# Cross-attention with 20 heads: the score tile from one product of 308 columns and two of 154, with a new order of steps in the slot

## The chip, the core and the metric

The kernel runs on one core of a Trainium2 chip. The metric is the device time of one execution, in microseconds (us). In what follows PE is TensorE, DVE is VectorE, ACT is ScalarE, POOL is GpSimd and SP is SyncE, whose queue issues the kernel's DMAs. PEld are the weight loads of TensorE.

## The reference

There are 32 batch elements, each with 512 query rows of 640 channels (`x`) and 77 context rows of 1024 channels. 20 heads have 32 channels each. Only the text part of the context has keys (77 of them), so the other three attentions of the full reference have no columns and add nothing.

```
q = heads(x @ to_q_w);  k = heads(ctx @ to_k_w);  v = heads(ctx @ to_v_w)
p = softmax(q @ k^T / sqrt(32))            # 512 x 77 for each head
out = merge(p @ v) @ to_out_w + to_out_b + x
```

All arrays are fp32.

## The kernel before

**Numbers in two parts.** TensorE multiplies in a shortened fp32 format (`fp32r`). To keep the accuracy, each operand is held as a high part and a low part: `split` (L100) copies the value into the shortened format on ACT (L101) and subtracts that copy from the value on DVE (L102). A product is then three TensorE products, high by high, high by low and low by high (`PAIRS`, L120), added up in PSUM.

**Stages.** A prologue computes keys and values for all 2464 context rows in five groups of up to 512 rows (`context`, `keys`, `context_values`, L133 to L208), and stores them with both parts in DRAM (`k_dram`, `v_dram`). The instructions of this prologue are ordered by a scheduler. The main part is written in a fixed order (`manual_schedule`, L657): what stands first in the program stands first on its engine's queue, and each engine works its queue in order.

**Slots.** The main part goes through 160 slots. Slot `n` belongs to batch element `b` and block `j` of four heads (five blocks in a batch element, `b, j = divmod(n, 5)`). `slot` (L523) mixes the work of several blocks so that TensorE always has something to do. For a block `n` these steps exist:

- `queries` (L316): 15 products of 512 columns give the transposed queries of the block, in one PSUM bank `pq`. `split_q` (L330) makes the high and low part `qt` of them: one ACT copy, one DVE subtraction. Both are done one slot ahead.
- `scores` (L334): for each of the four tiles of 128 query rows, three products of 308 columns (four heads of 77 keys). The moving operand `kb` holds the keys of each head in that head's 32 rows and zeros elsewhere, for both parts. After them DVE takes the maximum of each head (L348). There are three PSUM buffers for these tiles.
- `exps` (L353): four exponentials a tile on ACT (L358), with their sums.
- One slot later, `sums` (L366, a reciprocal on DVE), `normalize` (L371, a multiplication on POOL), and `transpose_p` (L377): a DVE transpose in 32 x 32 blocks into `z`, and four DMAs that write `z` to a DRAM tile `pd`.
- `load_p` (L393) reads `pd` back in the transposed layout as `raw`; three slots after the scores, `cast_p` (L400, ACT) and `rest_p` (L407: an ACT copy, a DVE subtraction at L411 with both operands in SBUF, a POOL subtraction at L414) make its two parts `pp`.
- `values` (L422): 8 products of 512 columns into `pa`, then `split_a` (L436).
- `piece` (L472) does 12 products of 320 columns of the output projection of the batch element before, twice a slot; `finish` (L480) adds residual and bias on DVE (L486) and stores the rows. `add_bias` (L450) adds the bias to the loaded residual on POOL.
- For the next batch element, `load_x` (L256) loads the rows, `transpose_x` (L264) transposes a quarter of them on DVE, and `split_x` (L268) makes the two parts of one of five blocks of channels: an ACT copy (L273) and a POOL subtraction (L274). Tables say in which slot of the five and at which of three places this is done: `TRANSPOSE_X` (L504) and `SPLIT_X` (L505).
- `refill` (L512) loads the keys and values of a batch element, in two groups of blocks (`load_keys` L295, `load_values` L304).

The order of the slot's steps by engine, before the change: DVE does the reciprocal, the first maximum, the subtraction of `rest_p`, the second maximum, output additions if there are any, the third maximum, the subtraction of `split_q`, the transpose of `p`, output additions, the fourth maximum and the subtraction of `split_a`. POOL does the subtraction of `rest_p`, `normalize`, the bias and the splits of `x`. From slot 4 on `values` are done, from slot 5 on the output projection. `end` (L594) finishes the last blocks.

Of the kernel before, what the change touches and what calls it, by code (L numbers as in the profile page):

```python
# [23 lines left out]
P = 128  # L24
# [26 lines left out]
def kernel(  # L51
# [22 lines left out]


    nc = tc.nc
    B, S, C = x.shape
# [83 lines left out]
    def keys(g0, gn, j, k):  # L161
        if k == 0:
            pks[j] = psk.tile([P, G], F32, tag="ps", name="pk")
        for n, (a, c) in enumerate(PAIRS):
            nc.tensor.matmul(  # L165
                pks[j][:, :gn],
                wk_s[:, k, a, j * P : (j + 1) * P],
                cts[k][:, c, :gn],
                start=(k == 0 and n == 0),
                stop=(k == NK - 1 and n == 2),  # L170
            )
        if k == NK - 1:
            pk = pks.pop(j)
            ks = kvt.tile([P, 2, G], FPR, tag="ks", name="ks")
            split(ks[:, 0, :gn], ks[:, 1, :gn], pk[:, :gn])
            nc.sync.dma_start(
                k_dram[:, j, :, g0 : g0 + gn].bitcast(F32), ks[:, :, :gn].bitcast(F32)
            )

# [88 lines left out]
    def split_x(b, c, engine=nc.gpsimd):  # L268

        xt = main.tile([P, 2, S], FPR, tag="xt", name="xt", bufs=8)  # L270
        src = xss[b].rearrange("p (a t) u -> p t a u", t=NQ)[:, :, :, c * Q : (c + 1) * Q]
        parts = [xt[:, i, :].rearrange("p (t a j) -> p t a j", t=NQ, j=Q) for i in range(2)]
        nc.scalar.copy(parts[0], src)  # L273
        engine.tensor_tensor(parts[1], src, parts[0].bitcast(F32), ALU.subtract)  # L274
        xts[b, c] = xt
# [4 lines left out]
    for g, (j0, nj) in enumerate(GROUPS):  # L280
        kb = main.tile([P, nj, 2, KCOLS], FPR, name=f"kb{g}")
        nc.gpsimd.memset(kb.bitcast(F32), 0.0)
        kbs.append(kb)
# [4 lines left out]
    qts = [main.tile([P, 2, S], FPR, name=f"qt{n}") for n in range(2)]  # L288
    z = main.tile([P, NBLK, NQ, Q], F32, name="z")
# [5 lines left out]
    def load_keys(b, g):  # L295
        j0, nj = GROUPS[g]
        for i in range(HPC):
            r = slice(i * HD, (i + 1) * HD)
            nc.sync.dma_start(
                kbs[g][r, :, :, i * NKEY : (i + 1) * NKEY].bitcast(F32),  # L300
                k_dram[r, j0 : j0 + nj, :, b * NKEY : (b + 1) * NKEY].bitcast(F32),
            )

    def load_values(b, g):  # L304
# [25 lines left out]
    def split_q(n):  # L330
        qt = qts[n % 2]
        split(qt[:, 0, :], qt[:, 1, :], pqs.pop(n))

    def scores(n, t):  # L334
        b, j = divmod(n, NC_)
        g = GROUP_OF[j]
        qt, kb = qts[n % 2], kbs[g][:, j - GROUPS[g][0]]
        sc = ps.tile([P, S], F32, tag="sc", name="sc", bufs=3)
        for m, (a, c) in enumerate(PAIRS):
            nc.tensor.matmul(  # L340
                sc[:, :KCOLS],
                qt[:, a, t * P : (t + 1) * P],
                kb[:, c, :],
                start=(m == 0),
                stop=(m == 2),
            )
# [89 lines left out]
    def split_a(n):  # L436
        if n >= N - NC_ + 1:
            at = main.tile([P, 2, S], FPR, tag="xt", name="at", bufs=8)
# [64 lines left out]
    BIAS = {2: (1, 0), 3: (1, 1), 4: (1, 2), 0: (2, 3)}  # L503
    TRANSPOSE_X = {0: ((), (0,), (1,)), 1: ((2,), (3,), ())}  # L504
    SPLIT_X = {1: ((), (0,)), 2: ((1,), (2,)), 3: ((3,), (4,))}  # L505
    wos = []
# [5 lines left out]
    def refill(b, j):  # L512

        if j == 0 and b >= 1:
            load_keys(b, 1)
        elif j == 1 and b >= 1:
            load_values(b, 0)
        elif j == 2 and b + 1 < B:
            load_keys(b + 1, 0)
        elif j == 3 and b >= 1:  # L520
            load_values(b, 1)

    def slot(n, beside=None):  # L523
# [133 lines left out]
    with tc.manual_schedule(engines=ENGINES):  # L657
        g0, gn = GROUPS_KV[-1]
        load_x(0)
        load_keys(0, 0)  # L660
        load_keys(0, 1)
        for g in range(2):
            load_values(0, g)
        for h in range(2):
# [69 lines left out]
```

## Time and profile before

| what | value |
|---|---|
| median of 3 runs | 2028.63 us (2027.86 to 2028.84) |
| the profiled execution's own time | 2028.15 us |
| its span, first to last instruction | 2026.0 us |
| mean granted TensorE clock | 0.991 of full speed |
| score products (L340) | 1920 of 308 columns, 377.8 us busy |
| projection products (L458) | 3840 of 320 columns, 615.9 us busy |
| query products (L322) | 2400 of 512 columns, 610.9 us busy |
| normalize (L373, POOL) | 160, mean 2276 ns |
| subtraction of rest_p (L411, DVE / L414, POOL) | 160 each, mean 1226 / 1770 ns |
| transpose of p (L380, DVE) | 160, mean 1511 ns |
| subtraction of split_q (L102, DVE) | 160, mean 684 ns |
| DMA over the span | 417.14 MB, mean 206 GB/s |

The page gives one execution. A busy time is the sum of an engine's instruction durations without overlaps, a mean is the duration of one instruction. The durations of matmuls overlap, since TensorE takes up the next before the last has drained, so their means are not their pace. In the timeline a line has the start, the duration, the engine, the line of the code, the operation with the tile it writes and the tiles it reads, the shapes, the count, and in brackets the engine's idle time just before, with what ended it.

### The profile page before, as it was taken

The numbers are of one execution on the slowest core, as the hardware profiler recorded it, in microseconds if no ns is written. First come the engines' busy times: TensorE is split into PE (matmuls) and PEld (weight loads), VectorE is DVE, ScalarE is ACT, GpSimd is POOL, SyncE is SP. The second block draws the span as 40 slices with busy tenths as digits, with TensorE's granted clock in tenths as the row PEclk, the third lists the DMA queues.
The fourth block names the chain that finished last, engine by engine and source line by source line (L and its number), as shares of the span: only waits on it lengthen the run. The fifth ranks groups of instructions, "written<-read, shape, count | busy, mean of one in ns | idle before, by whom it ended". The sixth has DMA issues, their size and how long they took to land.

```text
span 2026.0 us, 37077 instructions
## 1 busy us (share of the span) xinstructions
PE 1990.2 (98%) x11012; PEld 1802.7 (89%) x11012; DVE 1253.3 (62%) x1999; ACT 1397.0 (69%) x6057; POOL 1051.7 (52%) x615
## 2 busy tenths in 40 slices
PE   8899997999999999999999999999999999999998
PEld 7799986899999999999999999999999999999997
DVE  5443235566666666666666666666666666666663
ACT  3322127777778777777777777777778777787772
POOL 0000024666666666666656566666666666666654
PEclk9999998999999999999999999999999999999999
DMA  7963267988888888888888888888888887888865
GB/s 188 250 217 99 103 151 167 230 211 218 219 219 218 211 220 217 214 215 221 218 216 219 210 223 207 216 216 222 218 215 211 214 216 214 220 215 216 221 187 157
DMA packets 530212, 417.14 MB, mean 206 GB/s; under 512 B 144415, under 2 KB 433725, under 8 KB 530013
## 3 DMA queue, kind: packets, MB, share of 16 engines
q1 hardware_dynamic: 530013, 414.77, 78.7%
q8 instruction: 90, 1.47, 0.3%
q14 instruction: 109, 0.89, 0.1%
HBM read 239.30 MB, written 175.32 MB: 205 GB/s over the span
## 4 chain that ended last, share of the span: by engine, by line
PE 92%; DMA 3%; SPq 1%; ACT 1%; DVE 1%; issue 0%; POOL 0%; DVEq 0%; ACTq 0%; POOLq 0%
PE po L458 28%; PE pq L322 27%; PE pa L428 15%; PE sc L340 13%; PE pk L165 5%; PE pv L191 5%; DMA cs<-in_ctx_dram 1%; ACT pn L358 1%; DMA raw<-pd 0%; SPq L149 0%; SPq L111 0%; DVE z L380 0%; DMA xs<-in_x_dram 0%; DMA wraw<-in_L_xattn_to_out_w_dram 0%; SPq L387 0%
## 5 line engine op out<-in xcount | busy, mean ns | idle before, releaser
L358 ACT ACTIVATE pn<-sc,nm 128x77 f32<-128x77 f32 x2560 | 799.4, 329 | 105.1 <-DVE nm L348 101.4
L458 PE MATMUL po<-wo_s,at 128*128 128x320 f32 x3840 | 615.9, 310 | 5.2 <-DVE xr L486 5.2
L322 PE MATMUL pq<-xt,wq_s 128*128 128x512 f32 x2400 | 610.9, 395 | 0.0
L458 PEld LDWEIGHTS po<-wo_s,at 128*128 128x128 f32 x3840 | 576.5, 188 | 5.8 <-DVE xr L486 5.5
L414 POOL TENSOR_TENSOR pp<-raw,pp 64x512 fp32r<-64x512 f32 x160 | 283.2, 1770 | 512.5 <-ACT pp L410 510.0
L358 ACT ACTIVATION_READ_ACCUMULATOR pn<-sc,nm 128x1 f32 x2560 | 530.3, 207 | 0.0
L322 PEld LDWEIGHTS pq<-xt,wq_s 128*128 128x128 f32 x2400 | 437.3, 188 | 79.8
L348 DVE TENSOR_REDUCE nm<-sc 128x4 f32<-128x308 f32 x640 | 299.7, 469 | 297.0 <-PE sc L340 294.9
L373 POOL TENSOR_TENSOR pn<-pn,rs 128x1232 f32<-128x1232 f32 x160 | 364.1, 2276 | 33.1 <-DVE rs L368 20.9
L340 PE MATMUL sc<-kb,qt 128*128 128x308 f32 x1920 | 377.8, 306 | 2.4 <-ACT qt L101 1.7
L340 PEld LDWEIGHTS sc<-kb,qt 128*128 128x128 f32 x1920 | 325.4, 188 | 45.2 <-ACT qt L101 2.4
L428 PE MATMUL pa<-pp,vb 128*128 128x512 f32 x1280 | 331.5, 401 | 10.7 <-ACT pp L404 9.5
L380 DVE STREAM_TRANSPOSE z<-pn 128x1280 f32<-128x1280 f32 x160 | 241.8, 1511 | 78.8 <-POOL pn L373 29.4
L428 PEld LDWEIGHTS pa<-pp,vb 128*128 128x128 f32 x1280 | 246.0, 198 | 49.9 <-ACT pp L404 10.0
L274 POOL TENSOR_TENSOR xt<-xs,xt 128x512 fp32r<-128x512 f32 x157 | 202.6, 1294 | 149.0 <-ACT xt L273 145.6
L101 ACT CAST at<-pa 128x512 fp32r<-128x512 f32 x160 | 94.0, 588 | 256.8 <-PE pa L428 256.6
L411 DVE TENSOR_TENSOR pp<-raw,pp 128x1024 fp32r<-128x1024 f32 x160 | 196.1, 1226 | 50.6 <-ACT pp L404 50.3
L451 POOL TENSOR_TENSOR xr<-xr,bias 128x640 f32<-128x640 f32 x128 | 201.4, 1574 | 1.8 <-DMA xr<-in_x_dram 1.7
L404 ACT CAST pp<-raw 128x1024 fp32r<-128x1024 f32 x160 | 169.4, 1059 | 5.3 <-DMA raw<-pd 4.9
L165 PE MATMUL pk<-ct,wk_s 128*128 128x512 f32 (+1 forms) x600 | 137.8, 391 | 9.8 <-ACT ct L101 9.8
L191 PE MATMUL pv<-wv_s,ct 128*128 128x320 f32 (+1 forms) x960 | 143.6, 311 | 1.8 <-DVE vs L102 1.8
L191 PEld LDWEIGHTS pv<-wv_s,ct 128*128 128x128 f32 (+1 forms) x960 | 140.9, 186 | 4.0 <-DVE vs L102 2.1
(37 smaller groups left out, 1099.1 us busy)
## 6 DMA issues: line engine op xcount, KB each, us to landing
pd<-z SPq DMA_DIRECT2D x640, 160.0 KB, 3.8
raw<-pd SPq DMA_DIRECT2D x160, 512.0 KB, 4.2
xs<-in_x_dram SPq DMA_DIRECT2D x128, 320.0 KB, 7.5
xr<-in_x_dram SPq DMA_DIRECT2D x128, 320.0 KB, 4.7
out_dram<-xr SPq DMA_DIRECT2D x128, 320.0 KB, 3.5
raw<-pd SPq DMA_DIRECT2D x160, 128.0 KB, 4.4
v_dram<-vs SPq DMA_DIRECT2D x19, 640.0 KB, 3.7
k_dram<-ks SPq DMA_DIRECT2D x20, 512.0 KB, 3.3
```

The lines of the kernel that those rows point to most:

```text
L165: nc.tensor.matmul(pks[j][:, :gn], wk_s[:, k, a, j * P : (j + 1) * P], cts[k][:, c, :gn], start=(k == 0 and n == 0), stop=(k == NK - 1 and ...
L191: nc.tensor.matmul(pv[:tn, :HALF], cts[k][:, a, t0 : t0 + tn], wv_s[:, k, c, h * HALF : (h + 1) * HALF], start=(k == 0 and n == 0), stop=( ...
L274: engine.tensor_tensor(parts[1], src, parts[0].bitcast(F32), ALU.subtract)
L322: nc.tensor.matmul(pqs[n], wq_s[:, k, a, j * P : (j + 1) * P], xts[b, k][:, c, :], start=(k == 0 and m == 0), stop=(k == NC_ - 1 and m == 2),)
L340: nc.tensor.matmul(sc[:, :KCOLS], qt[:, a, t * P : (t + 1) * P], kb[:, c, :], start=(m == 0), stop=(m == 2),)
L348: nc.vector.tensor_reduce(nm, sc[:, :KCOLS].rearrange("p (h k) -> p h k", k=NKEY), AX.X, ALU.max, negate=True)
L358: nc.scalar.activation(pnb[n % 2][:, at, :NKEY], sc[:, i * NKEY : (i + 1) * NKEY], AF.Exp, bias=nm[:, i : i + 1], accum_out=sms[n][:, at : ...
L373: nc.gpsimd.tensor_tensor(pf, pf, rs.unsqueeze(2).to_broadcast([P, NQ * HPC, NKEY]), ALU.mult)
L380: nc.vector.transpose(z.rearrange("p b t j -> p t b j"), pn.rearrange("p (t h) k -> p t (h k)", t=NQ).rearrange("p t (b i) -> p t b i", i=Q),)
L414: nc.gpsimd.tensor_tensor(pp[64:, 4, :], raw[:64, 2, :], pp[:64, 4, :].bitcast(F32), ALU.subtract)
L428: nc.tensor.matmul(pas[n], vb[:, t, :, a], pp[:, c, :], start=(m == 0), stop=(m == len(PASSES) - 1),)
L458: nc.tensor.matmul(pos[b, t, h][:, :HALF], ats[b * NC_ + j][:, a, t * P : (t + 1) * P], wos[0][:, j, c, h * HALF : (h + 1) * HALF], start= ...
```

## The change

**Scores.** The second and third product of a score tile now cover two heads each, 154 columns, and use all 128 rows: 64 rows hold the low part of the queries of two heads against the high part of their keys, the other 64 the high part of the same queries against the low part of the keys. For this there is a second tile of keys, `kc`, beside `kb`; `kb` now has high parts only. `load_keys` issues a DMA for each of the two, per head: eight in place of four. `k_dram` holds the parts in the rows that `kc` needs, so that each block of keys is stored by four DMAs in place of one (`keys`).

**split_q.** `qt` has three parts: the high part in all rows, and two mixed parts. ACT makes the first as before. For each mixed part DVE subtracts in 64 rows, and copies the high part of those rows into the other 64.

**Order in the slot.** `normalize` stands ahead of `rest_p`, so on POOL too. `transpose_p`, with its four DMAs, stands ahead of the second group of exponentials, that is on DVE ahead of the third maximum and of `split_q`, where it stood behind both. `finish` stands ahead of the second `transpose_x`. The tables for `x` are changed: the transposes are spread over slots 0 to 2 of the five, the splits over slots 2 and 3 (two and three of them) in place of 1 to 3. `xt` has seven buffers in place of eight. The keys and values of the first batch element beyond the first group are loaded in the slots, not ahead of them.

```diff
             split(ks[:, 0, :gn], ks[:, 1, :gn], pk[:, :gn])
-            nc.sync.dma_start(
-                k_dram[:, j, :, g0 : g0 + gn].bitcast(F32), ks[:, :, :gn].bitcast(F32)
-            )
+            for w in range(2):
+                for half in range(2):
+                    nc.sync.dma_start(
+                        k_dram[half * 64 : half * 64 + 64, j, w, g0 : g0 + gn].bitcast(F32),
+                        ks[w * 64 : w * 64 + 64, int(half != w), :gn].bitcast(F32),
+                    )
...
     def load_keys(b, g):
         j0, nj = GROUPS[g]
+        kb, kc = kbs[g]
+        src = k_dram[:, j0 : j0 + nj, :, b * NKEY : (b + 1) * NKEY].bitcast(F32)
         for i in range(HPC):
-            r = slice(i * HD, (i + 1) * HD)
+            r, half = slice(i * HD, (i + 1) * HD), i % 2 * NKEY
             nc.sync.dma_start(
-                kbs[g][r, :, :, i * NKEY : (i + 1) * NKEY].bitcast(F32),
-                k_dram[r, j0 : j0 + nj, :, b * NKEY : (b + 1) * NKEY].bitcast(F32),
-            )
+                kb[r, :, i * NKEY : (i + 1) * NKEY].bitcast(F32), src[r, :, i // 2, :]
+            )
+            nc.sync.dma_start(kc[r, :, :, half : half + NKEY].bitcast(F32), src[r])
...
     def split_q(n):
-        qt = qts[n % 2]
-        split(qt[:, 0, :], qt[:, 1, :], pqs.pop(n))
+
+        qt, pq = qts[n % 2], pqs.pop(n)
+        nc.scalar.copy(qt[:, 0, :], pq)
+        lower, upper = slice(0, 64), slice(64, P)
+        for w, (r, other) in enumerate(((lower, upper), (upper, lower))):
+            nc.vector.tensor_tensor(
+                qt[r, 1 + w, :], pq[r], qt[r, 0, :].bitcast(F32), ALU.subtract
+            )
+            nc.vector.tensor_copy(qt[other, 1 + w, :], qt[r, 0, :].bitcast(F32))
...
         sc = ps.tile([P, S], F32, tag="sc", name="sc", bufs=3)
-        for m, (a, c) in enumerate(PAIRS):
+        half = KCOLS // 2
+        for m, (cols, keys_) in enumerate(
+            (
+                (slice(0, KCOLS), kb[:, jg]),
+                (slice(0, half), kc[:, jg, 0]),
+                (slice(half, KCOLS), kc[:, jg, 1]),
+            )
+        ):
             nc.tensor.matmul(
-                sc[:, :KCOLS],
-                qt[:, a, t * P : (t + 1) * P],
-                kb[:, c, :],
+                sc[:, cols],
+                qt[:, m, t * P : (t + 1) * P],
+                keys_,
...
-    TRANSPOSE_X = {0: ((), (0,), (1,)), 1: ((2,), (3,), ())}
-    SPLIT_X = {1: ((), (0,)), 2: ((1,), (2,)), 3: ((3,), (4,))}
+    TRANSPOSE_X = {0: ((), (0,), ()), 1: ((1,), (2,), ()), 2: ((3,), (), ())}
+    SPLIT_X = {2: ((0,), (1,)), 3: ((2, 3), (4,))}
...
         s = scores(n, 0)
+        if n:
+            normalize(n - 1, rs)
         if taken is not None:
             rest_p(taken)
-        if n:
-            normalize(n - 1, rs)
         exps(n, 0, *s)
...
             add_bias(b - BIAS[j][0], BIAS[j][1])
+        if n:
+            transpose_p(n - 1)
         exps(n, 1, *s)
...
         exps(n, 2, *s)
-        if n:
-            transpose_p(n - 1)
         for c in xsplits[0]:
             split_x(b + 1, c)
         if has_out:
             piece(bo_, first)
+        finish()
         for i in turns[1]:
             transpose_x(b + 1, i)
-        finish()
```

In the changed file the lines have moved: `normalize` is L398, the subtractions of `rest_p` are L436 (DVE) and L439 (POOL), the subtractions and copies of `split_q` are L346 and L349, the score products L365 and the maximum L373, the transpose of `p` L405, the output additions L511 and the reciprocal L393.

More of the change, by code (lines that the diff above doesn't have):

```diff
@@ L268, in split_x @@
     def split_x(b, c, engine=nc.gpsimd):
-        xt = main.tile([P, 2, S], FPR, tag="xt", name="xt", bufs=8)
+        xt = main.tile([P, 2, S], FPR, tag="xt", name="xt", bufs=7)
         src = xss[b].rearrange("p (a t) u -> p t a u", t=NQ)[:, :, :, c * Q : (c + 1) * Q]
@@ L280 @@
     for g, (j0, nj) in enumerate(GROUPS):
-        kb = main.tile([P, nj, 2, KCOLS], FPR, name=f"kb{g}")
-        nc.gpsimd.memset(kb.bitcast(F32), 0.0)
-        kbs.append(kb)
+        kb = main.tile([P, nj, KCOLS], FPR, name=f"kb{g}")
+        kc = main.tile([P, nj, 2, KCOLS // 2], FPR, name=f"kc{g}")
+        for tile_ in (kb, kc):
+            nc.gpsimd.memset(tile_.bitcast(F32), 0.0)
+        kbs.append((kb, kc))
     for n in range(2):
@@ L287 @@
         pnb.append(pn)
-    qts = [main.tile([P, 2, S], FPR, name=f"qt{n}") for n in range(2)]
+    qts = [main.tile([P, 3, S], FPR, name=f"qt{n}") for n in range(2)]
     z = main.tile([P, NBLK, NQ, Q], F32, name="z")
@@ L336, in scores @@
         g = GROUP_OF[j]
-        qt, kb = qts[n % 2], kbs[g][:, j - GROUPS[g][0]]
+        qt, (kb, kc) = qts[n % 2], kbs[g]
+        jg = j - GROUPS[g][0]
         sc = ps.tile([P, S], F32, tag="sc", name="sc", bufs=3)
-        for m, (a, c) in enumerate(PAIRS):
+        half = KCOLS // 2
[6 more added lines that the diff above has]
+        ):
             nc.tensor.matmul(
-                sc[:, :KCOLS],
-                qt[:, a, t * P : (t + 1) * P],
-                kb[:, c, :],
+                sc[:, cols],
+                qt[:, m, t * P : (t + 1) * P],
+                keys_,
                 start=(m == 0),
@@ L437, in split_a @@
         if n >= N - NC_ + 1:
-            at = main.tile([P, 2, S], FPR, tag="xt", name="at", bufs=8)
+            at = main.tile([P, 2, S], FPR, tag="xt", name="at", bufs=7)
         else:
@@ L512, in refill @@
     def refill(b, j):
-        if j == 0 and b >= 1:
+        if j == 0:
             load_keys(b, 1)
-        elif j == 1 and b >= 1:
+        elif j == 1:
             load_values(b, 0)
@@ L519, in refill @@
             load_keys(b + 1, 0)
-        elif j == 3 and b >= 1:
+        elif j == 3:
             load_values(b, 1)
@@ L660 @@
         load_keys(0, 0)
-        load_keys(0, 1)
-        for g in range(2):
-            load_values(0, g)
         for h in range(2):
```

## The prediction

> **What bounds the kernel now.** I read the page first (busy shares, chain), then the windows of the steady part, then the timeline of one slot on each engine, then the one place where VectorE and GpSimd meet on SBUF.
>
> ```profile
> PE 1990.2 (98%) x11012; PEld 1802.7 (89%) x11012; DVE 1253.3 (62%) x1999; ACT 1397.0 (69%) x6057; POOL 1051.7 (52%) x615
> ...
> PE 92%; DMA 3%; SPq 1%; ACT 1%; DVE 1%; issue 0%; POOL 0%; DVEq 0%; ACTq 0%; POOLq 0%
> PE po L458 28%; PE pq L322 27%; PE pa L428 15%; PE sc L340 13%; PE pk L165 5%; PE pv L191 5%; DMA cs<-in_ctx_dram 1%; ACT pn L358 1%; DMA raw<-pd 0%; SPq L149 0%; SPq L111 0%; DVE z L380 0%; DMA xs<-in_x_dram 0%; DMA wraw<-in_L_xattn_to_out_w_dram 0%; SPq L387 0%
> ```
>
> The end is set by PE, and score products (L340) are 13% of the chain. The records give PE's real pace as start-to-start distances: 142 ns for a product of 308 columns, 148 for 320, 233 for 512. A slot (one batch element, one block of four heads) is 15 x 233 + 12 x 142 + 8 x 235 + 24 x 148 ns = 10.6 us. Five slots take 52.95 us by the repeat of the trace, so in the steady part nothing but PE counts, and the first question is who is next. One slot on VectorE and on GpSimd:
>
> ```profile
> 1002.96 0.25 DVE L368 RECIPROCAL rs<-sm 128x16 f32<-128x16 f32 x1 [0.81 <-ACT pn L358]
> ...
> 1003.90 1.23 DVE L411 TENSOR_TENSOR pp<-raw,pp 128x1024 fp32r<-128x1024 f32 x1 [0.36 <-ACT pp L404]
> 1005.05 0.47 DVE L348 TENSOR_REDUCE nm<-sc 128x4 f32<-128x308 f32 x1
> 1005.43 0.48 DVE L486 TENSOR_TENSOR xr<-po,xr 128x320 f32<-128x320 f32 x1
> 1006.64 0.48 DVE L348 TENSOR_REDUCE nm<-sc 128x4 f32<-128x308 f32 x1 [0.72 <-PE sc L340]
> 1007.41 0.69 DVE L102 TENSOR_TENSOR qt<-pq,qt 128x512 fp32r<-128x512 f32 x1 [0.29 <-ACT qt L101]
> 1008.67 1.51 DVE L380 STREAM_TRANSPOSE z<-pn 128x1280 f32<-128x1280 f32 x1 [0.57 <-POOL pn L373]
> 1010.70 0.48 DVE L348 TENSOR_REDUCE nm<-sc 128x4 f32<-128x308 f32 x1 [0.52 <-PE sc L340]
> ```
> ```profile
> 1004.50 1.78 POOL L414 TENSOR_TENSOR pp<-raw,pp 64x512 fp32r<-64x512 f32 x1 [1.69 <-ACT pp L410]
> 1006.37 2.27 POOL L373 TENSOR_TENSOR pn<-pn,rs 128x1232 f32<-128x1232 f32 x1
> ```
>
> VectorE waits here for PE, with half a microsecond to spare. The reader is to see two more things. L414 starts while L411 runs and ends 1.15 us after L411's end (1006.28 against 1005.13); so it is in all 160 pairs, also where it started earlier (then it took 1.90 instead of 1.77). GpSimd is held while a VectorE operation with two SBUF operands runs. The reverse stands once, in the prologue:
>
> ```profile
> 280.94 0.69 DVE L274 TENSOR_TENSOR xt<-xs,xt 128x512 fp32r<-128x512 f32 x1 [0.69 <-ACT xt L273]
> 281.99 3.05 DVE L274 TENSOR_TENSOR xt<-xs,xt 128x512 fp32r<-128x512 f32 x2 [0.35 <-ACT xt L273]
> ...
> 281.51 2.98 POOL L274 TENSOR_TENSOR xt<-xs,xt 128x512 fp32r<-128x512 f32 x2 [7.16 <-ACT xt L273]
> ```
>
> The same VectorE subtraction takes 0.69 us alone, and 1.37 and 1.75 when a GpSimd one was there first: each ends 0.55 us after GpSimd's end, that is, it runs whole from 0.13 us before that end. Operations with one SBUF operand (L380 at 1008.67 beside L451) are not slowed.
>
> **The change, part by part. Score products.** 308 + 154 + 154 columns in place of 3 x 308. No product under 308 columns is in the trace. Bounds: 142 ns each (nothing won), and by the slope (233 - 142)/204 = 0.45 ns a column, 73 ns. Between them lies the weight load. At 295.73 a score product that found PE empty took 411 ns instead of 303, and the next weight load began 107 ns in: a load of 128 columns occupies 108 ns, and in the records each load begins 3 ns after the product ahead of it. So a short product cannot be followed sooner than 110 ns. The Trainium skill (TensorE: Matmul & The Clock Gate, Back-to-back issue gap) gives about 81 ns for a load and product pair of 128 columns. By that a tile wins 2 x 61 ns, 78 us over 640 tiles; by the row 2 x 32 to 34 ns, 41 to 44 us. I take the row: PE's slot falls from 10.59 to 10.31 us.
>
> **split_q.** One subtraction of 0.68 us becomes two of 64 x 512 from PSUM and two SBUF copies of 64 x 512. Length counts, not partitions, so 0.68 each for the subtractions. No VectorE copy is in the trace. The nearest row, 512 elements at 0.68, is the upper bound. The skill (VectorE: DVE Perf Modes, The perf-mode tier table) says that an fp32 copy within SBUF runs two elements a cycle (1227 ns for 2048); less its half of the work, 512 come to an estimated 0.42. By the one the slot's VectorE gains 2.0 us, by the other 1.5. I take 0.42, since source and target are plain contiguous rows, and keep 0.68 for the range. Neighbours overlap by 0.08 us in the trace; the same page's section on two instructions with no wait between them says that one starting on another quadrant is held to the end of the last, which these four would be: 0 to 0.3 us a slot, taken as 0.
>
> **New order.** normalize (L373) now precedes rest_p on GpSimd, and the transpose of p (L380) moves ahead of the third reduction. I follow the loop that VectorE's order closes, from one reciprocal to the next, by the rows above (start-to-start where operations follow on). Reciprocal at 0; normalize 0.40 to 2.68. rest_p's subtraction (L411) is ready at 0.94, as before, but GpSimd is now inside normalize: held to 2.55, done at 3.78. Behind it in VectorE's order: reduction 3.70, transpose 4.09, reduction 5.53, split_q 5.92 to 7.80 (0.60 + 0.34, twice), last reduction to 8.28. From there to the next reciprocal 1.40 us (1001.56 to 1002.96: four exponentials). Loop: 9.68 us. Eight additions (L486, 0.38) and four transposes of x (0.75) in five slots add 1.21 a slot: 10.89, against PE's 10.31. Before, L411 ran at once, normalize came after it and the transpose after that; the same sum gives about 9.0 + 1.0 us, under PE's 10.6, as the idle times show.
>
> Small terms a batch element: ScalarE does x splits between the third exponentials and the last, now two in slot 2 and three in slot 3 (0.6 each), which with the later third reduction puts it behind VectorE by 0.5 and 0.3 us; GpSimd's last x split runs 0.4 us into slot 4's normalize. Five slots: 54.4 + 1.2 = 55.6 us, 2.65 more than 52.95. Slots 4 to 159 have all of it, 31.2 batch elements: +83 us. PE's 43 us then lie idle: PE waits at each slot's first score tile for split_q.
>
> **The rest.** First four slots: no rest_p, loop 8.4 to 9.9 against 7.6 to 8.0 (reciprocals 312.87, 320.49, 328.52), and split_q(0) is 1.5 us longer with PE waiting: +5 us; less, if 14 value loads taken out of the start free SP. k_dram: 100 issues for 25, the same packets; the next loads queue behind them on SP, where PE stood 6 us at 69 (0 to +5; with SP's relief later I take 0). Key loads: 8 more issues in five slots at 0.6 us (four took 2.42), and 640 packets of 308 bytes at 23 ns over 16 DMA engines, 0.9 us a batch element on an 84% share. Queued behind is raw<-pd (4.2 us to land), due at the next slot's cast; VectorE's transpose is earlier, so SP reaches the key loads earlier, with some 4 us over. Zero; without that cover 2 us in two of five slots. xt with 7 buffers: the oldest are read by PE before their turn, zero.
>
> Sum: 2028.15 + 83 + 5 = 2116 us (span 2026.0 and 2 us around it; the median of the runs is 0.5 higher).
>
> **Rivals.** *PE stays the bound (faster).* If a subtraction behind normalize is not held as at 281.99, L411 ends at 2.17, the transpose starts at 2.70, and the loop is 8.3 + 1.2 = 9.5 us, under 10.31. Then 43 us come off and 5 are lost: 1990. For it: one place in the trace shows the hold in this direction. Against: three operations there alternate to 0.01 us, and 160 pairs show the other direction. It decides where the loop passes 10.3 us. *Copies at full length.* 0.52 us more a slot, 2.6 per batch element: 2116 + 81 = 2197; for it the nearest row, against it the page. It stays on the same side. *Holds between quadrants* add 1.6 per batch element: 2166; without the small terms 2078. That is the likeliest case's own range, 2078 to 2166.
>
> **Numbers.** Loop with the hold 0.60; copies at full length or held behind GpSimd 0.15; a loop near PE's pace, 2000 to 2070, 0.08; PE bound 0.17. The range leaves out the last and the far ends: 2035 to 2220. Faster by over 0.2% (what a measurement of this kernel can tell) 0.18, within 0.03, slower 0.79.
>
> **What would show it.** L436 (the former L411) with a mean near 2.8 us instead of 1.23, beginning while L398 runs; PE idle before L365 released by VectorE's L346 or L349; five slots of 55 to 56 us; products of 154 columns 110 ns apart; L439's mean still near 1.15 after L436. An L436 of 1.23 refutes the hold, and then the time is near 1990. Copies of 0.68 give 2200.

## The result and the profile after

The changed kernel takes 2178.87 us (2172.95 to 2181.77) against 2027.76 us for the kernel before in the same runs: the ratio is 1.074, 95% interval 1.0724 to 1.0756. It is slower. The forecast was 2116 us with a range of 2035 to 2220. The profiled execution took 2178.22 us, 150.1 more than the profiled execution of before.

The page of the changed kernel first: busy shares, then the chain of work that ended last, by engine and by line.

```profile
PE 2019.7 (93%) x11012; PEld 1768.6 (81%) x11012; DVE 1722.1 (79%) x2479; ACT 1376.7 (63%) x6057; POOL 1123.9 (52%) x617
...
DMA 24%; DVE 21%; PE 20%; SPq 13%; issue 13%; ACT 7%; POOL 2%; DVEq 0%; POOLq 0%; ACTq 0%
DMA pd<-z 10%; DVE z L405 5%; PE pq L332 5%; DVE nm L373 4%; SPq L412 4%; ACT pn L383 4%; PE po L483 4%; PE pv L197 4%; DVE qt L346 4%; PE pk L168 4%; SPq L319 3%; DVE xr L511 3%; DVE qt L349 2%; DMA vb<-v_dram 2%; PE sc L365 2%
```

PE was 92% of the chain and is 20% now. VectorE has 469 us more busy time, and the writes of `z` with their issue (`pd<-z`, L412) stand in the chain with 14%, where they had less than 1% before. The groups that the change touches, from the table of groups by shape (busy us, mean ns of one):

```profile
L436 DVE TENSOR_TENSOR pp<-raw,pp 128x1024 fp32r<-128x1024 f32 x160 | 454.0, 2838 | 59.9 <-ACT pp L429 59.9
...
L439 POOL TENSOR_TENSOR pp<-raw,pp 64x512 fp32r<-64x512 f32 x160 | 342.5, 2140 | 42.3 <-ACT pp L435 30.1
...
L346 DVE TENSOR_TENSOR qt<-pq,qt 64x512 fp32r<-64x512 f32 x320 | 218.4, 682 | 12.0 <-ACT qt L343 3.1
L349 DVE CAST qt<-qt 64x512 fp32r<-64x512 f32 x320 | 135.0, 422 | 4.3
```

L436 took 1226 ns before (as L411) and takes 2838 now, the same work. One slot (the fourth of its five) on VectorE, then GpSimd. The first VectorE line and the PE line belong to the end of the slot before: a copy, and the score product that waits for it.

```profile
1085.34 0.42 DVE L349 CAST qt<-qt 64x512 fp32r<-64x512 f32 x1
...
1087.73 0.25 DVE L393 RECIPROCAL rs<-sm 128x16 f32<-128x16 f32 x1 [0.73 <-ACT pn L383]
...
1088.66 2.81 DVE L436 TENSOR_TENSOR pp<-raw,pp 128x1024 fp32r<-128x1024 f32 x1 [0.35 <-ACT pp L429]
1091.39 0.47 DVE L373 TENSOR_REDUCE nm<-sc 128x4 f32<-128x308 f32 x1
1091.78 1.50 DVE L405 STREAM_TRANSPOSE z<-pn 128x1280 f32<-128x1280 f32 x1
...
1093.75 0.68 DVE L346 TENSOR_TENSOR qt<-pq,qt 64x512 fp32r<-64x512 f32 x1
1094.44 0.42 DVE L349 CAST qt<-qt 64x512 fp32r<-64x512 f32 x1
1094.88 0.69 DVE L346 TENSOR_TENSOR qt<-pq,qt 64x512 fp32r<-64x512 f32 x1
1095.59 0.42 DVE L349 CAST qt<-qt 64x512 fp32r<-64x512 f32 x1
...
1098.72 0.25 DVE L393 RECIPROCAL rs<-sm 128x16 f32<-128x16 f32 x1 [0.81 <-ACT pn L383]
```
```profile
1088.12 2.27 POOL L398 TENSOR_TENSOR pn<-pn,rs 128x1232 f32<-128x1232 f32 x1
1090.47 2.16 POOL L439 TENSOR_TENSOR pp<-raw,pp 64x512 fp32r<-64x512 f32 x1
```
```profile
1085.82 0.34 PE L365 MATMUL sc<-kc,qt 128*128 128x154 f32 x1 [0.82 <-DVE qt L349]
```

L436 starts 0.54 us after the normalisation L398 did, and ends at 1091.47, 1.08 us after L398's end at 1090.39. Its own length is 1.23 us, so it ran whole from 0.15 us before that end. This is called a hold below: an operation has begun by its record, but gets on only when that of the other engine is through. Everything behind L436 on VectorE stands in one closed row, down to `split_q`, and PE waits at a score product for the copy L349. L439, in turn, starts while L436 runs and ends 1.16 us after it. Over the whole run PE is idle 77.5 us ahead of the short score products L365 (69.1 of them until an L349 ends), 31.0 us ahead of L483 until an output addition frees its bank, and 26.4 us ahead of L453, half of it until an L436 ends.

The time from one reciprocal to the next, as mean over the steady part (500 to 1900 us of each trace), for the five slots of a batch element. The forecast's column is worked out from its own terms: 9.68, plus 0.38 for each output addition and 0.75 for each transpose of x in that slot, plus its small terms of 0.5, 0.3 and 0.4 in slots 2, 3 and 4.

| slot | before | forecast | after |
|---|---|---|---|
| 0 | 11.48 | 10.81 | 11.67 |
| 1 | 10.26 | 11.94 | 12.21 |
| 2 | 10.12 | 11.31 | 11.21 |
| 3 | 10.58 | 10.74 | 10.99 |
| 4 | 10.52 | 10.84 | 11.31 |
| sum | 52.95 | 55.64 | 57.40 |

The steady part is 4.45 us a batch element longer, times 31.2 gives 139 us. Slot 4 begins 12.8 us later (the fill), the tail is about 1 us shorter: 151 us, against 150 measured.

### The profile page after: what moved, and what is told of

Same layout as the page of the kernel before. It is cut to its first block, busy times and chain, and to the rows that moved or that the text cites. A ratio compares the mean times of both kernels' runs of the same rounds, so it can differ in the third digit from the quotient of the medians.

```text
span 2176.5 us, 37872 instructions
## 1 busy us (share of the span) xinstructions
PE 2019.7 (93%) x11012; PEld 1768.6 (81%) x11012; DVE 1722.1 (79%) x2479; ACT 1376.7 (63%) x6057; POOL 1123.9 (52%) x617
## 4 chain that ended last, share of the span: by engine, by line
DMA 24%; DVE 21%; PE 20%; SPq 13%; issue 13%; ACT 7%; POOL 2%; DVEq 0%; POOLq 0%; ACTq 0%
DMA pd<-z 10%; DVE z L405 5%; PE pq L332 5%; DVE nm L373 4%; SPq L412 4%; ACT pn L383 4%; PE po L483 4%; PE pv L197 4%; DVE qt L346 4%; PE pk L168 4%; SPq L319 3%; DVE xr L511 3%; DVE qt L349 2%; DMA vb<-v_dram 2%; PE sc L365 2%
## 5 line engine op out<-in xcount | busy, mean ns | idle before, releaser
L398 POOL TENSOR_TENSOR pn<-pn,rs 128x1232 f32<-128x1232 f32 x160 | 364.4, 2278 | 591.1 <-DVE rs L393 591.0
L483 PE MATMUL po<-wo_s,at 128*128 128x320 f32 x3840 | 634.6, 313 | 31.0 <-DVE xr L511 31.0
L332 PE MATMUL pq<-xt,wq_s 128*128 128x512 f32 x2400 | 622.9, 401 | 0.0
L483 PEld LDWEIGHTS po<-wo_s,at 128*128 128x128 f32 x3840 | 565.8, 188 | 39.8 <-DVE xr L511 39.4
L436 DVE TENSOR_TENSOR pp<-raw,pp 128x1024 fp32r<-128x1024 f32 x160 | 454.0, 2838 | 59.9 <-ACT pp L429 59.9
L453 PE MATMUL pa<-pp,vb 128*128 128x512 f32 x1280 | 347.9, 406 | 26.4 <-DVE pp L436 13.5
L439 POOL TENSOR_TENSOR pp<-raw,pp 64x512 fp32r<-64x512 f32 x160 | 342.5, 2140 | 42.3 <-ACT pp L435 30.1
L365 PEld LDWEIGHTS sc<-kc,qt 128*128 128x128 f32 x1280 | 218.0, 189 | 135.7 <-DVE qt L349 110.5
L365 PE MATMUL sc<-kc,qt 128*128 128x154 f32 x1280 | 256.1, 267 | 77.5 <-DVE qt L349 69.1
L453 PEld LDWEIGHTS pa<-pp,vb 128*128 128x128 f32 x1280 | 240.5, 198 | 86.8 <-DVE pp L436 34.9
L373 DVE TENSOR_REDUCE nm<-sc 128x4 f32<-128x308 f32 x640 | 283.9, 444 | 6.7 <-PE sc L365 5.6
L405 DVE STREAM_TRANSPOSE z<-pn 128x1280 f32<-128x1280 f32 x160 | 239.6, 1498 | 22.9 <-POOL pn L398 8.9
L346 DVE TENSOR_TENSOR qt<-pq,qt 64x512 fp32r<-64x512 f32 x320 | 218.4, 682 | 12.0 <-ACT qt L343 3.1
L365 PE MATMUL sc<-kb,qt 128*128 128x308 f32 x640 | 196.3, 307 | 3.2 <-ACT pn L383 1.4
```

The lines of the kernel that those rows point to most:

```text
L332: nc.tensor.matmul(pqs[n], wq_s[:, k, a, j * P : (j + 1) * P], xts[b, k][:, c, :], start=(k == 0 and m == 0), stop=(k == NC_ - 1 and m == 2),)
L346: nc.vector.tensor_tensor(qt[r, 1 + w, :], pq[r], qt[r, 0, :].bitcast(F32), ALU.subtract)
L365: nc.tensor.matmul(sc[:, cols], qt[:, m, t * P : (t + 1) * P], keys_, start=(m == 0), stop=(m == 2),)
L373: nc.vector.tensor_reduce(nm, sc[:, :KCOLS].rearrange("p (h k) -> p h k", k=NKEY), AX.X, ALU.max, negate=True)
L398: nc.gpsimd.tensor_tensor(pf, pf, rs.unsqueeze(2).to_broadcast([P, NQ * HPC, NKEY]), ALU.mult)
L405: nc.vector.transpose(z.rearrange("p b t j -> p t b j"), pn.rearrange("p (t h) k -> p t (h k)", t=NQ).rearrange("p t (b i) -> p t b i", i=Q),)
```

## The experiments

Times are medians, each with its ratio to the kernel before run on the same chip, and the 95% interval. "Sum" is the sum of the five slots as in the table above.

**1. Which part of the order costs what.** First the kernel before with the two moves alone: normalisation ahead of `rest_p`, transpose of `p` ahead of the second exponentials. Scores and `split_q` stay as they were.

```diff
         s = scores(n, 0)
+        if n:
+            normalize(n - 1, rs)
         if taken is not None:
             rest_p(taken)
-        if n:
-            normalize(n - 1, rs)
...
+        if n:
+            transpose_p(n - 1)
         exps(n, 1, *s)
...
         exps(n, 2, *s)
-        if n:
-            transpose_p(n - 1)
```

> The kernel before with only the new order: normalize ahead of rest_p, the transpose of p ahead of the second exponentials; score products, split_q, key loads and the tables for x as before. Theory (the hold behind normalize costs, but only as a term of VectorE's loop): the subtraction of rest_p is held here too, mean near 2.75 us in place of 1.23, but split_q is short (0.6 us in the loop in place of 2.3), so the loop is about 3.7 + 0.4 + 1.4 + 0.4 + 0.6 + 0.5 + 1.4 = 8.4 us plus 1.2 for additions and x transposes = 9.6, under TensorE's 10.6: no change within 0.3%, 2028 us. Rival (the order alone makes the kernel slower): 2070 or more.

Measured: 2054.34 us, ratio 1.0115 (1.0093 to 1.0137), sum 53.93. The groups of this kernel, where L411 is the subtraction of `rest_p` and L380 the transpose:

```profile
L411 DVE TENSOR_TENSOR pp<-raw,pp 128x1024 fp32r<-128x1024 f32 x160 | 425.5, 2660 | 65.8 <-ACT pp L404 65.4 <-DMA vb<-v_dram 0.2
L380 DVE STREAM_TRANSPOSE z<-pn 128x1280 f32<-128x1280 f32 x160 | 239.8, 1499 | 126.1 <-DMA pd<-z 102.3 <-POOL pn L373 10.7 <-DMA kb<-k_dram 8.2
```

The hold is there in full (2660 ns against 1226) and shows in no slot but the first: slots 1 to 4 take 10.62, 10.41, 10.01 and 9.46 us, slot 0 takes 13.44. There the transpose waits for the writes of the `z` of the slot before, 4.0 us in the mean (1.3 us in the kernel before). So the hold alone stays covered by VectorE's spare time, and the early transpose has a price that neither theory had: there is one buffer `z`, and in the last slot of a batch element the loads of x stand ahead of `z`'s writes on SP's queue. No run took this wait out of this kernel.

Next, the changed kernel with the normalisation alone put back behind `rest_p`:

```diff
-        if n:
-            normalize(n - 1, rs)
         if taken is not None:
             rest_p(taken)
+        if n:
+            normalize(n - 1, rs)
```

> The changed kernel with normalize put back behind rest_p on GpSimd, and nothing else. Theory: the subtraction of rest_p runs at once (1.23 us) and GpSimd's one waits for it, but the early transpose of p must now wait for normalize, which ends at about 5.7 us after the reciprocal: 5.7 + 1.4 + 0.4 + 2.3 + 0.5 + 1.4 = 11.7 us plus 1.2, slower than the changed kernel by some 1.2 us a slot, 2330 to 2370 us. Rival (the place of normalize is what costs the time, and the transpose has room): about 2060 to 2110.

Measured: 2361.34 us, ratio 1.1635 (1.1616 to 1.1654), sum 63.29, as the theory expected. L436 has a mean of 1225 ns. The hold is gone, and the transpose stands on VectorE ahead of all that it could do meanwhile, waiting for a normalisation that GpSimd only starts once its own part of `rest_p` is done:

```profile
L405 DVE STREAM_TRANSPOSE z<-pn 128x1280 f32<-128x1280 f32 x160 | 241.9, 1512 | 457.1 <-POOL pn L398 450.8 <-DMA kc<-k_dram 6.3
```

The two moves belong together: with the early transpose, the early normalisation is worth 182 us, its hold on L436 included. Then both moves undone in the changed kernel, so that only scores, `split_q`, keys and tables differ from before (the diff is the two of above, reversed):

> The changed kernel with both moves undone: normalize behind rest_p, the transpose of p behind split_q. split_q's two VectorE copies now fall into normalize's time. Theory [...]: the first copy is held to the end of normalize, 5.6 us after the reciprocal, means of the copies well over 0.42 us, loop about 11 us plus 1.2: 2130 to 2230. Rival (the copies are not held): loop about 9 + 1.0, TensorE bound at 10.3 us a slot, 1990 to 2000 us.

Measured: 2241.45 us, ratio 1.1042 (1.1023 to 1.1061), sum 59.37. The rival is refuted; the theory's range is missed by 11 us. Its groups:

```profile
L349 DVE CAST qt<-qt 64x512 fp32r<-64x512 f32 x320 | 265.2, 829 | 4.3
...
L436 DVE TENSOR_TENSOR pp<-raw,pp 128x1024 fp32r<-128x1024 f32 x160 | 196.0, 1225 | 62.0 <-ACT pp L429 62.0
```

The hold has moved: L436 is free, and the copies take 829 ns in the mean instead of 422. In its timeline the first copy begins while the normalisation runs in four of the five slots, and takes some 820 ns. The second begins while the bias addition runs in three of them, and takes some 970; where GpSimd is idle it takes 423. The new order alone is therefore not what made the kernel slow: it is 63 us better than the old order for this `split_q`. What costs is the longer `split_q` together with a hold on VectorE, and each order has one.

**2. Is the hold of L436 decisive?** The changed kernel with L436 as a pass of the same size that reads one operand. It leaves out the subtraction, so the low part of `p` is missing from its result:

```diff
-        nc.vector.tensor_tensor(
-            pp[:, 2:4, :], raw[:, 0:2, :], pp[:, 0:2, :].bitcast(F32), ALU.subtract
-        )
+        nc.vector.tensor_reduce(
+            pp[:, 2:4, :], raw[:, 0:2, :].unsqueeze(3), AX.X, ALU.max
+        )
```

> The changed kernel with one edit: VectorE's subtraction in rest_p (L436, two operands from SBUF) becomes a VectorE pass of the same size that reads only one operand (pp's middle rows get a copy of raw, so the low part of p is wrong; order, sizes and readers are the same). Theory (L436 lasts 2.84 us because its second operand from SBUF waits for GpSimd's normalisation): the pass takes 1.1 to 1.3 us, VectorE's chain in the slot loses 1.5 us, and the slot falls back to TensorE's own 10.3 to 10.7 us: 1995 to 2060 us. Rival (the order of the queue and not the hold makes the slot long): the pass still ends at about 3.8 us after the reciprocal and the time stays at 2150 to 2180 us.

Measured: 2058.64 us, ratio 1.0154 (1.0131 to 1.0176), sum 53.68. Its groups:

```profile
L436 DVE TENSOR_REDUCE pp<-raw 128x1024 fp32r<-128x1024 f32 x160 | 192.7, 1204 | 0.6 <-DMA raw<-pd 0.6
...
L405 DVE STREAM_TRANSPOSE z<-pn 128x1280 f32<-128x1280 f32 x160 | 241.9, 1512 | 176.7 <-DMA pd<-z 92.8 <-POOL pn L398 40.0 <-DMA kc<-k_dram 28.3
```

The pass starts beside the normalisation (0.50 us after the reciprocal) and takes 1204 ns: with one operand GpSimd doesn't hold it. 120 of the 151 us that the change cost go with it, and the rival is refuted. The run takes away two more things: the pass no longer waits for ScalarE's cast, so it starts 0.44 us earlier than L436 did (0.50 in place of 0.94), and it no longer holds L439 (1.29 us in place of 2.14). Of the 2.1 us by which it ends earlier, some 1.6 are the hold. So the hold is the largest cause, though the 120 us are not all its own. What is left is slot 0, 13.51 us with 4.3 us of wait for DMAs ahead of its transpose; the other four slots take 10.47, 9.50, 10.67 and 9.52.

**3. Are the copies the rest?** The changed kernel without `split_q`'s two copies. Their halves of `qt` are set to zero once, so the scores lack the products of the queries' high parts with the keys' low parts:

```diff
-            nc.vector.tensor_copy(qt[other, 1 + w, :], qt[r, 0, :].bitcast(F32))
```

> The changed kernel without the two copies of split_q (the upper halves of the score operand are cleared once and never filled, so the scores lack the products of the high parts with the keys' low parts). Theory (VectorE's chain bounds the slot, and the copies cost 0.42 us each and 0.02 us between): 0.9 us a slot less where VectorE bounds, 160 slots: 2178 minus 110 to 145, 2033 to 2070 us. Rival (another engine is close behind and takes over at once): 2100 us or more.

Measured: 2120.15 us, ratio 1.0459 (1.0443 to 1.0474), sum 55.92. This is the rival's side: 59 us come off, not 110 to 145. Slot 1 loses 0.87 us, what the copies took, and slot 3 0.46. Slot 4 loses 1.48, more than the copies took, because there the hold turns round:

```profile
1014.36 1.23 DVE L437 TENSOR_TENSOR pp<-raw,pp 128x1024 fp32r<-128x1024 f32 x1 [0.36 <-ACT pp L430]
...
1014.43 3.29 POOL L399 TENSOR_TENSOR pn<-pn,rs 128x1232 f32<-128x1232 f32 x1
```

GpSimd is late there with its last split of x, so the subtraction of `rest_p` (L437 here) begins 0.07 us ahead of the normalisation. It takes its 1.23 us, and the normalisation takes 3.29 in place of 2.28. This is so in all 30 slots of this run in which the subtraction begins first. So the one that begins later is held, with code, operands and sizes unchanged. The same shows in slot 1 of the run with the loads of x moved (part 5): there L436 begins only after the normalisation has ended, and takes 1.22 us in 22 of the 24 slots of the steady part.

Slot 2 stays at 11.21: VectorE now waits there for ScalarE, which does two splits of x. Slot 0 gets longer by 1.34: VectorE arrives earlier at its transpose, which waits 2.7 us for the writes of `z`. A shorter VectorE queue is given back at the next limit in two of five slots.

**4. Copies elsewhere, in the old order.** Three ways to take copies out of GpSimd's reach (the diffs leave out the lines of part 1 that give the old order). First one copy from PSUM on ScalarE and one from PSUM on VectorE, in place of two in SBUF:

```diff
-            nc.vector.tensor_copy(qt[other, 1 + w, :], qt[r, 0, :].bitcast(F32))
+            if w == 0:
+                nc.scalar.copy(qt[other, 1 + w, :], pq[r])
+            else:
+                nc.vector.tensor_copy(qt[other, 1 + w, :], pq[r])
```

> As the one before (old order), and the two copies of split_q read the queries from PSUM in place of SBUF, one on ScalarE (0.6 us) and one on VectorE (0.68 us)[...]. Theory: nothing is held, VectorE's loop is 9.7 to 10 us, TensorE bounds again with its shorter score tile (110 ns after each product of 154 columns): 1985 to 2005 us, faster than both kernels. Rival (VectorE or ScalarE is simply too full with the new split_q, whatever the order): 2060 or more.

Measured: 2202.19 us, ratio 1.0847 (1.0826 to 1.0868), sum 57.96. The theory fell. From the waits of this kernel over the steady part (us in total, times, longest):

```profile
ACT qt L350 <- DVE qt L346: 98.6, 130, 0.8
...
DVE qt L346 <- ACT qt L350: 83.8, 130, 0.6
```

Subtraction, ScalarE's copy and second subtraction wait for one another in turn, and the whole takes 3.4 us. It starts only 4.43 us after the reciprocal (median), when ScalarE's cast of `qt` is through, and the transpose stands behind it. So the second try has the subtractions back to back, and both copies on ScalarE behind the third exponentials:

```diff
-            nc.vector.tensor_copy(qt[other, 1 + w, :], qt[r, 0, :].bitcast(F32))
...
+    def copy_q(n):
+        qt, pq = qts[n % 2], pqs.pop(n)
+        nc.scalar.copy(qt[64:, 1, :], pq[:64])
+        nc.scalar.copy(qt[:64, 2, :], pq[64:])
...
         exps(n, 2, *s)
+        if n:
+            transpose_p(n - 1)
+        if ahead:
+            copy_q(n + 1)
```

> The changed kernel with the order of before for the normalisation, split_q's two half subtractions back to back on VectorE, and the two copies on ScalarE from PSUM behind the third exponentials and behind the transpose of p. Theory: no copy waits in VectorE's queue and none can be held by GpSimd; ScalarE has 1.2 us more a slot at 63% busy; TensorE bounds again or nearly: 10.3 to 10.6 us a slot, 2000 to 2040 us. Rival (ScalarE's late copies are what the next slot's first score waits for, or they hold the one PSUM buffer of q too long for the next queries): 2080 us or more.

Measured: 2097.24 us, ratio 1.0345 (1.0319 to 1.0371), sum 54.94: the fastest of the kernels that have the new products and leave nothing out, and still slower than before. Slots 2 to 4 take 9.99, 10.66 and 9.70. Slot 0 takes 12.80, with 2.4 us of wait for the writes of `z`, and slot 1 takes 11.79, with 1.7 us ahead of the subtraction of `rest_p`, which waits for ScalarE's cast of `p`. Last, both copies as DMAs on SP's queue:

```diff
-            nc.vector.tensor_copy(qt[other, 1 + w, :], qt[r, 0, :].bitcast(F32))
+            nc.sync.dma_start(qt[other, 1 + w, :].bitcast(F32), qt[r, 0, :].bitcast(F32))
```

> The changed kernel with the order of before (normalisation behind rest_p, transpose of p after the third exponentials) and split_q's two copies made by two DMAs on SP's queue, from the high part in SBUF to the other half. VectorE then has no copy that GpSimd can hold, and its queue holds only the two half subtractions. Theory (TensorE's 154-column products do save their 0.25 us a slot, and VectorE's queue took it back): TensorE bounds again, 10.1 to 10.4 us a slot, 1990 to 2025 us, at or just under the kernel before. Rival (the DMAs land late or delay p's reads on SP): TensorE waits for them at the first score of the next slot, 2060 us or more.

Measured: 2430.56 us, ratio 1.1992 (1.1962 to 1.2022), sum 65.46. The rival was right, and too mild. Ahead of slot 0 the two copies are issued on SP right behind five loads of 320 KB each (four of x and one of the residual), at 1072.37 in the timeline of this kernel, and PE gets the first of them 9 us later:

```profile
1081.53 0.82 PE L365 MATMUL sc<-kc,qt 128*128 128x154 f32 x2 [6.99 <-DMA qt<-qt]
```

Slot 0 alone takes 19.43 us; over all slots the median from issue to landing is 5.0 us.

**5. The wait for z's writes.** Could the order on SP remove it? The loads of x are put behind the transpose of `p`, first in the changed kernel:

```diff
-        if j == 4 and b + 2 < B:
-            load_x(b + 2)
...
         if n:
             transpose_p(n - 1)
+        if j == 4 and b + 2 < B:
+            load_x(b + 2)
         exps(n, 1, *s)
```

> The changed kernel with one edit: in the last slot of a batch element the loads of x stand on SP's queue behind the four writes of z instead of ahead of them. Theory (the extra 0.4 us that the mean slot 0 waits with its transpose of p is the writes of z standing behind those loads): the wait ends, 0.4 us less per batch element and some of the 1.4 us in the slots where it is longest: 2150 to 2172 us. Rival (the wait has another source, or the later x makes its first transpose late): no change or slower, 2173 us or more.

Measured: 2186.56 us, ratio 1.0789 (1.0773 to 1.0806), sum 57.67. Slot 0 loses its 0.40 us and becomes regular (11.27 in all batch elements). Slot 1 gets 0.68 longer: now the reads of `p` stand behind the loads of x. The waits of this kernel over the steady part show the chain, from the read to the cast on ScalarE and from that to L436:

```profile
DVE pp L436 <- ACT pp L429: 103.9, 130, 3.7
...
ACT pp L429 <- DMA raw<-pd: 54.8, 28, 3.3
```

So the rival holds: the source of the wait was rightly named, but in the new place too the loads of x delay what stands behind them. The same edit in the kernel before and in the kernel with ScalarE's copies (there the loads stand behind the later transpose):

> The kernel before with the same edit of SP's order. There slot 0 waits 1.3 us for the writes of z. Theory (TensorE bounds the kernel before, so a wait on VectorE is mostly covered): 2010 to 2028 us. Rival (the wait in slot 0 reaches TensorE): 0.9 us in each of 32 batch elements, 1990 to 2005 us.

Measured: 2029.09 us, ratio 1.0007 (0.9999 to 1.0016), no difference, as good as what the theory expected. Slot 0 no longer waits for `z`, but 2.6 us for its first transpose of x; the sum stays (53.02).

> The kernel with the copies on ScalarE and the order of before for the normalisation, and in addition the x loads behind the writes of z. In the run without this edit slot 0 waited 2.4 us for the writes of z and slot 1 waited 1.4 us for the cast of p behind it; the other slots took 9.7 to 10.7 us. Theory (that wait is all that keeps it above the kernel before, and TensorE's 154-column products do save time): five slots of 51.0 to 52.5 us, 1980 to 2025 us, under the kernel before. Rival (ScalarE with 1.2 us more a slot bounds, or the products save nothing): 2030 us or more.

Measured: 2158.24 us, ratio 1.0642 (1.0627 to 1.0656), sum 56.92. The theory fell: slot 0 takes 12.56, now with 2.1 us ahead of the transpose of x, and slot 1 takes 13.82, where L440, the subtraction of `rest_p`, stands 3.8 us idle behind ScalarE's cast of a `p` that comes late.

**6. L436 on the other engine.** The last try moves the subtraction of `rest_p` to GpSimd, makes the copies one-operand reductions, and puts the transpose back behind the third exponentials:

```diff
-            nc.vector.tensor_copy(qt[other, 1 + w, :], qt[r, 0, :].bitcast(F32))
+            nc.vector.tensor_reduce(
+                qt[other, 1 + w, :], qt[r, 0, :].bitcast(F32).unsqueeze(2), AX.X, ALU.max
+            )
...
-        nc.vector.tensor_tensor(
+        nc.gpsimd.tensor_tensor(
             pp[:, 2:4, :], raw[:, 0:2, :], pp[:, 0:2, :].bitcast(F32), ALU.subtract
```

> The changed kernel with three edits: rest_p's subtraction of 128x1024 moves from VectorE to GpSimd behind the normalisation, so that VectorE has no two-operand pass from SBUF for GpSimd to hold; split_q's two copies become one-operand reductions over an axis of length 1 (by the run with one operand such a pass is not held by GpSimd); and the transpose of p stands behind the third exponentials as in the kernel before, so that slot 0 waits less for the writes of z. Theory: VectorE loses 2.84 us a slot and pays 0.3 us more for the copies, GpSimd has 2.0 us more a slot (2.28 us for 1232 elements in the normalisation), 8 to 10 us a slot, 11 us in slot 3 with its three splits of x; TensorE or GpSimd bound at 10.3 to 10.7 us a slot: 2000 to 2070 us. Rival (GpSimd's low part comes too late for the products with the values, or its queue passes 10.6 us a slot): 2090 us or more.

Measured: 2213.92 us, ratio 1.0904 (1.0874 to 1.0933), sum 58.15. The rival was right. GpSimd takes 2.39 us for this subtraction, behind the normalisation, and the products with the values wait for it (groups of this kernel; L455 are the value products):

```profile
L455 PE MATMUL pa<-pp,vb 128*128 128x512 f32 x1280 | 404.3, 438 | 121.8 <-POOL pp L438 108.3 <-ACT pp L431 13.4
...
L438 POOL TENSOR_TENSOR pp<-raw,pp 128x1024 fp32r<-128x1024 f32 x160 | 381.9, 2387 | 29.5 <-ACT pp L431 28.6 <-PE po L485 0.8
```

The reductions take 680 ns each where the copies took 422, and are as long beside GpSimd as without it.

## Why the prediction was right in kind and short in size

**The mechanism held.** That VectorE's loop takes the place of PE as the bound, with the hold of L436 as its largest term, is what the traces show. L436 was forecast near 2.8 us and has 2838 ns. PE waits at L365 for L349. L439 was forecast to end 1.15 us after L436, and ends 1.16 after it. That the hold costs is shown by the run that takes it away (2058.64 us), and that it is a hold by the 30 slots of the run without copies in which the subtraction began first. That it costs *here* and not in general is shown by the kernel before with the new order alone, where L411 is held nearly as long (2660 ns) and slots 1 to 4 take 10.12 us in the mean, within PE's pace: the hold and the 1.6 us that `split_q` has more are each nearly affordable, together they are not.

**Score products: right.** By the starts of PE's records, a tile takes 425 ns before, from its first product to the first of the next group. After, it takes 324, but then the first product of the next group keeps PE some 40 ns longer (188 in place of 148 where that is a product of 320 columns). Together that is 61 ns by 640 tiles, 39 us, against 41 to 44 forecast. The loads that follow on the two short products start 108 and 111 ns after the load before. The row carried here; the 81 ns of the Trainium skill (TensorE: Matmul & The Clock Gate, Back-to-back issue gap) would have made it 78 us. That a kernel can pocket the 39 us isn't shown: in none of the runs with the new products was PE alone the bound.

**Copies: right.** 422 ns against 0.42 us estimated from the Trainium skill (VectorE: DVE Perf Modes, The perf-mode tier table); the nearest row in the trace, 0.68, was the wrong guide here. The same page's rule (Two Vector instructions with no wait between them) was then not followed where it should have been: **"held to the end of the last, which these four would be: 0 to 0.3 us a slot, taken as 0"** is the step that failed first. In the timeline the four of `split_q` follow each other with gaps of 13 to 31 ns where other neighbours overlap by 80 (and one reduction starts 70 ns before the transpose ends). In the loop `split_q` costs 2.30 us, not 1.88: 0.42 a slot, 2.1 a batch element. The gaps agree with the page's rule; no run moves these operations onto one quadrant, so the cause is not shown by itself. Setting an unknown with a stated rule behind it to the end that the rule speaks against was a choice, not a reading.

**The transpose's place: incomplete.** The forecast asked what the earlier transpose waits for on GpSimd, and found the normalisation. It counted SP's queue only for what the transpose's own DMAs push back ("Zero"). It did not ask whether `z`, of which there is one, is free. In slot 0 it is not: 0.40 us in the mean. This is small in the changed kernel because L436 is late there. Where VectorE reaches the early transpose sooner, the wait is 4.0 us (new order alone) and 4.3 us (one operand). By the slots it is what makes the new order alone slower (by 24.8 us).

**Small terms: half right.** ScalarE's 0.5 and 0.3 us in slots 2 and 3 disappear beside the longer `split_q` (0 and about 0.1 are left): two limits of nearly the same length are not to be added. The run without copies shows ScalarE's: slot 2 stays at 11.21 with 0.8 us less on VectorE. The last split of x does run into slot 4, where L436 takes 3.31 us: 0.47, forecast 0.4.

The account of a batch element: +2.1 for `split_q`, +0.4 for `z`, -0.7 for ScalarE's terms, make 1.8 us, 55 us over the run. The fill cost 12.8 us instead of 5; of what it is made was not tried. 55 + 8 - 1 is the 62 us between 2116 and 2178.

**The rivals.** "PE stays the bound" gave 1990 us for a L436 that isn't held. The trace refuted its cause; the one-operand run shows that even without the hold the time is 2059, with the wait for `z` in slot 0, so its price was 69 us too low as well. "Copies at full length" fell with the 422 ns. "Holds between quadrants", 2166 us, was the rival nearest to the result, and the gaps fit it.

**What stays open.** No version was found that beats the kernel before. Two buffers for `z`, which should take the wait of slot 0 away with no change on SP, were not tried; whether they fit into SBUF isn't shown. The tables for x, the seven buffers of `xt` and the split key loads are in every run with the new products, and no run undid them alone.

## What to carry to other kernels

A VectorE subtraction with two operands in SBUF, or a VectorE copy within SBUF, took turns here with GpSimd's passes over SBUF, and the one that began later was held. Put such operations in the timeline as one queue, and before adding a copy to VectorE ask which GpSimd pass stands beside it: in this kernel moving the normalisation only moved the hold, from the copies to L436. When PE is the bound by about half a microsecond a slot, a change that saves PE 0.3 us and costs another engine 1.6 us is lost before any detail is known. When a step is moved earlier, check the buffer that it writes as well as the data that it reads: the wait for its last reader may stand behind a large load on a queue.

## What the runs showed of the hardware that was not expected

- The hold depends on the form, not on the engine: a VectorE pass of 128x1024 beside GpSimd's normalisation took 2838 ns as a subtraction of two SBUF operands and 1204 ns as a reduction of one. A copy of 64x512 within SBUF, though it has one operand, took 422 ns where no GpSimd pass was under way when it began, and some 820 ns behind the normalisation. The Trainium skill (SBUF — State Buffer, Who interferes with whom) has all three: a VectorE instruction with two SBUF inputs contends with a GpSimd one that reads SBUF, a copy in the fast mode takes ports that GpSimd needs, and a reduction never contends. The runs agree. It also says that the issue order decides who waits, and so it was in the 30 slots of the run without copies where the subtraction began first (1.23 us, the normalisation some 3.28).
- The price of not being held: as reductions the copies take 680 ns, 258 more than as copies.
- A small DMA within SBUF on a queue with other traffic took 5.0 us in the median to land at 128 KB, longer than the 4.4 us that the reads of `p` of 512 KB took in the same run.
- The mean granted clock was lowest where PE waited most: 0.932 in the run whose score products waited for the copying DMAs, 0.954 in the run with the normalisation put back, against 0.989 in the changed kernel and 0.991 in the kernel before.
